# Gathered rows of a graph network summed as three bf16 parts in two half visits, with two blocks fewer gathered

## The chip, the cores and the metric

The kernel runs on one core of one Trainium2 chip. The time is the device time of one execution in microseconds; of the kernel before three runs are on record.

## The reference

The network has 6250 nodes with 256 features and 100000 directed edges. After a layer norm with a ReLU come four layers; in each, every node adds up the rows of its neighbours, and a small perceptron follows:

```python
def agg(h):
    return jax.ops.segment_sum(h[src], dst, num_segments=N)
for l in range(NL - 1):
    h = x + agg(x)
    h = jax.nn.relu(h @ W1s[l] + b1s[l])
    h = jax.nn.relu(h @ W2s[l] + b2s[l])
    x = h @ W3s[l] + b3s[l]
h = x + agg(x)
h = jax.nn.relu(h @ cW1 + cb1)
h = jax.nn.relu(h @ cW2 + cb2)
return h @ cW3 + cb3
```

The input is added to the result at the end. Everything is float32. The edges are the same in all layers and come sorted by `dst`.

## The kernel before

The nodes stand in 49 blocks of 128. In the code, layers are numbered from 0; the text says layer 1 to layer 4, so that layer 1 is `l == 0`. The aggregation of a block of destination nodes is made in one of two ways.

**Dense blocks.** For them a matrix of edge counts (uint8) is built once, in layer 1, out of one-hot matmuls in bf16 (L1271), and stored in HBM. In layers 2 to 4 it is fetched back (`at<-mat`), cast to fp32r tiles `a` by ScalarE and VectorE in turn (L1853; layer 1: L1836), and multiplied on TensorE with the node table `XY`, which holds a high and a low part of each row. Four blocks together make a panel: 49 steps of four matmuls of 512 columns (`agg<-a,XY`, L1962). A panel of three blocks has 384 columns. A block by itself (a solo) takes 49 matmuls of 512 columns with the table as the weights (`agg<-XY,a`, L1877). The tiles `a` come from a ring, so the casts run some steps ahead of TensorE.

**Gathered blocks.** The class `Gathered` holds them, 24, 22, 21 and 19 blocks in the four layers. A block's edges are 16 tiles of 128 edges, and what does not fit there lies in a tile `over` that several blocks share. For each tile an indirect DMA from GpSimd's queue reads the 128 rows of the table that its edges start from (`rows`, issued in `send`, L1631). VectorE builds one-hot matrices `hot` (L1673), one per block. A visit of a block (`add`) sums its tiles on TensorE: every tile is multiplied with a 128x32 one-hot (L1692) into one of four groups of 32 output partitions, which TensorE works on at once. In fp32 each matmul stands in the trace as two records. VectorE then adds the block's own rows (`finish`, L1716 and L1719), TensorE transposes the result (`turned`, L1758), and the perceptron follows (L1448, L1511).

**What sets the order.** The program is written out by a planner. It walks over the steps of the dense product and keeps an estimated time, `clock`, to which each piece of work adds its cost (`VISIT` is 3.0 us, `TURN` 0.4). The gathers of a layer are spread evenly over it (`pace`), each bound to a matmul of TensorE that must have passed; `meets` says when the next visit is due, `TAIL` and `LATE` shift the end of a layer's visits against the end of its dense product. `later(n, f)` writes `f` n steps on. Every engine runs its instructions in the order in which they were written.

**Where the change acts.** In the class `Gathered`, in the two pools of layers 2 to 4 (`rings2` for the tiles `a`, `gath2` for the gathered tiles), and in the tables that say which blocks are dense (`solos`, `slim`, `order`).

Of the kernel before, what the change touches and what calls it, by code (L numbers as in the profile page):

```python
# [17 lines left out]
P = 128  # L18
# [378 lines left out]
def sorted_edges(  # L397
# [61 lines left out]
    ROUNDS = ((3, 1, -1, 0, 4, 2),)  # L459
    CH = 7  # L460
# [12 lines left out]
    solos = [[], [], [], [18, 19]]  # L473
    slim = {1: 1}
# [681 lines left out]
    with tc.manual_schedule():  # L1156
# [157 lines left out]
        def later(n, fn):  # L1314
            due.append((now[0] + n, fn))
# [88 lines left out]
        def bring_inputs(b0, n):  # L1404

            assert layers[NLAYER].sent == len(layers[NLAYER].order)
            assert layers[NLAYER].done == layers[NLAYER].n
            inputs[b0] = [gath.tile([P, C], F32, name="rows") for _ in range(n)]
# [153 lines left out]
        class Gathered:  # L1562
            def __init__(self, l):
# [12 lines left out]
                self.visits = [(g, rounds) for g in range(len(self.blocks)) for rounds in ROUNDS]  # L1576
# [4 lines left out]
                seen_over = set()  # L1581
                for g, rounds in self.visits:
                    b = self.blocks[g][0] + self.blocks[g][2]
                    new = [T] if over_of[b] not in seen_over else []
                    seen_over.add(over_of[b])
                    used_at = {k: i for i, c in reversed([*enumerate(rounds)])
                               for k in range(c, T + 1, 4) if k in (*range(own[b]), *new)}
                    assert len(used_at) == own[b] + len(new)
                    self.order += [(g, k) for k in sorted(used_at, key=lambda k: (used_at[k], k))]
                    self.upto.append(len(self.order))  # L1590

            def meets(self):
# [21 lines left out]

            def send(self, upto):
                while self.sent < min(upto, len(self.order)):
                    g, k = self.order[self.sent]
                    which = over_of[self.blocks[g][0] + self.blocks[g][2]]
                    if k == T:
                        t = gath.tile([P, C], F32, name="over", bufs=2)  # L1620
                        self.shared[which] = t
                        at = late_ends[:, which, 1:2]
                    else:
# [3 lines left out]
                        t = gath.tile([P, C], F32, name="rows")  # L1627
                        self.rows[g, k] = t
# [9 lines left out]
            def advance(self):  # L1638

                if self.first is None:  # L1640
                    return
                self.flow()
                while self.meets():
                    self.send(self.upto[self.done + 1])
                    self.add()
# [10 lines left out]
            def one_hots(self, v):  # L1656
# [5 lines left out]
                if which not in known:  # L1662
                    known.add(which)
                    m = P // Q - 1
                    c = T - 4 * m - min(rounds)
# [5 lines left out]
                shape = [P, len(rounds), P // Q, Q]  # L1671
                self.hot = work.tile(shape, F32, name="hot")
                nc.vector.tensor_tensor(  # L1673
                    self.hot,
                    sums[:, C:C + P].rearrange("p (m q) -> p m q", q=Q)[:, None, :, :].to_broadcast(shape),
                    rel[:, self.blocks[g][3] // T, v % len(ROUNDS), :, :, None].to_broadcast(shape),
                    OP.is_equal)

            def add(self):
# [5 lines left out]
                end = rounds == ROUNDS[-1]  # L1685
                held_by = [[c for c in rounds if 0 <= c + 4 * m < own[b + i] or c + 4 * m == T]
                           for m in range(P // Q)]
                for c in rounds:
                    for m, cs in enumerate(held_by):
                        if c in cs:  # L1690
                            k = c + 4 * m
                            nc.tensor.matmul(  # L1692
                                self.sums[m * Q:(m + 1) * Q, :C],
                                self.hot[:, c - min(rounds), m, :],
                                self.shared[over_of[b + i]] if k == T else self.rows[g, k],
                                start=(c == cs[0]), stop=(c == cs[-1]))
                passed(VISIT)
                self.done += 1
                if self.done < self.n:
                    later(4, lambda v=self.done: self.one_hots(v))  # L1700
# [68 lines left out]
        order = [[], [0, 1, 2, 3, 4, 5, 6], [0, 1, 2, 3, 4, 5, 6], [0, 18, 1, 2, 19, 3, 4, 5, 6]]  # L1769
# [32 lines left out]
        def work_of(l):  # L1802
# [3 lines left out]
            t += len(layers[l].blocks) * (len(ROUNDS) * VISIT + TURN)  # L1806
# [210 lines left out]
        rings = ctx.enter_context(tc.tile_pool(name="rings2", bufs=AHEAD + 5, reuse_waits="tile"))  # L2017
        gath = ctx.enter_context(tc.tile_pool(name="gath2", bufs=27, reuse_waits="tile"))
# [69 lines left out]
```

## Time and profile before

| what | value |
| --- | --- |
| median of three runs | 2338.97 us (2338.20 to 2346.93) |
| the profiled execution | 2345.17 us |
| its span in the trace | 2343.4 us |
| TensorE busy | 2136.8 us, 91% |
| layer 1 / 2 / 3 / 4 in the trace | 92 to 755 / 755 to 1320 / 1320 to 1846 / 1846 to 2343 us |
| blocks gathered in layers 1 / 2 / 3 / 4 | 24 / 22 / 21 / 19 |
| mean granted TensorE clock | 0.973 |

The busy share is that of one engine in the span, and the engines work beside each other. A row of a group reads: line, engine, operation, what is written from what, shape, count, then busy time, the mean of one in ns, and after the second bar the idle time of that engine just before those instructions with what ended it; "issue" there is idle time in which the engine waited for nothing that the profile shows. Matmuls overlap, so the mean of one is longer than the step from one to the next; steps are read from the starts in the timeline.

### The profile page before, as it was taken

What the parts mean: (1) busy time and instruction counts of PE and PEld (TensorE: products, weight loads), DVE (VectorE), ACT (ScalarE), POOL (GpSimd) and SP (SyncE); (2) the same over time, 40 slices, a digit from 0 to 9 for tenths busy, and PEclk for the clock granted to TensorE, in tenths of its full rate; (3) what the DMA queues carried; (4) which work ended last, traced back from release to release, by engine and by line L of the source; (5) the groups of instructions that cost most, each with busy time, mean ns of one, the idle gap of its engine ahead of it and who ended that gap; (6) DMA issues with size and microseconds to landing.
All of it is one profiled execution on the core that took longest, in us unless ns stands there. A gap on an engine that the chain in (4) does not pass through costs nothing.

```text
span 2343.4 us, 33115 instructions
## 1 busy us (share of the span) xinstructions
PE 2136.8 (91%) x12131; PEld 1517.0 (65%) x12131; DVE 909.0 (39%) x2079; ACT 839.3 (36%) x1738; POOL 1398.1 (60%) x1479
## 2 busy tenths in 40 slices
PE   7988898988899999899998999999999999999998
PEld 6766566656567666576666766666666766666665
DVE  8777565666543321222224322222223322322223
ACT  6755454444445322222233322222222422222221
POOL 4466666665551666666666466666666366666664
PEclk9999999999899999999999999999999999999999
DMA  8444444443444644444445544545445554545454
GB/s 240 161 141 129 131 133 122 137 144 119 126 141 138 205 143 121 138 151 145 135 146 184 175 137 118 161 127 156 127 142 179 173 156 151 172 152 178 140 154 125
DMA packets 184921, 348.81 MB, mean 149 GB/s; under 512 B 31785, under 2 KB 118699, under 8 KB 184749
## 3 DMA queue, kind: packets, MB, share of 16 engines
q0 software_dynamic: 68256, 185.33, 27.4%
q1 hardware_dynamic: 115944, 159.42, 20.8%
q10 hardware_dynamic: 548, 1.86, 0.3%
q8 instruction: 97, 1.59, 0.3%
q14 instruction: 76, 0.61, 0.1%
HBM read 287.62 MB, written 58.87 MB: 148 GB/s over the span
## 4 chain that ended last, share of the span: by engine, by line
PE 84%; issue 6%; DVE 3%; another core or an unknown queue 3%; ACT 2%; DMA 1%; POOL 1%; SPq 0%; ACTq 0%; POOLq 0%; DVEq 0%
PE agg L1962 39%; PE sums L1692 14%; PE agg L1877 12%; PE ps L1448 5%; PE ps L1511 5%; PE bp L1271 4%; PE bp L1089 1%; PE ps L1758 1%; DMA rows<-table,idx 1%; DVE hi L1233 1%; DVE at L1281 1%; PE ps L1460 1%; PE ps L1440 0%; POOL rows L1631 0%
## 5 line engine op out<-in xcount | busy, mean ns | idle before, releaser
L1631 POOL DMA_INDIRECT rows<-table,idx x1368 | 1324.5, 968 | 866.2 <-PE agg L1962 279.0
L1962 PE MATMUL agg<-a,XY 128*128 128x512 f32 (+1 forms) x4116 | 986.6, 396 | 11.9 <-issue 5.8
L1962 PEld LDWEIGHTS agg<-a,XY 128*128 128x128 f32 x4116 | 770.4, 190 | 210.3 <-issue 55.2
L1853 ACT CAST a<-at 128x512 fp32r<-128x512 uint8 (+1 forms) x529 | 314.5, 612 | 728.0 <-PE agg L1962 558.2
L1853 DVE CAST a<-at 128x512 fp32r<-128x512 uint8 (+1 forms) x528 | 235.9, 458 | 635.0 <-PE agg L1962 385.0
L1692 PE MATMUL sums<-rows,hot 128*32 128x256 f32 x3768 | 344.3, 391 | 73.8 <-issue 61.5
L1877 PE MATMUL agg<-XY,a 128*128 128x512 f32 x1323 | 384.7, 423 | 3.4 <-issue 1.1
L1692 PEld LDWEIGHTS sums<-rows,hot 128*32 128x32 f32 x3768 | 145.3, 111 | 253.8 <-issue 193.6
L1877 PEld LDWEIGHTS agg<-XY,a 128*128 128x128 f32 x1323 | 240.5, 197 | 47.4 <-issue 6.5
L1279 ACT CAST at<-bp 128x392 uint8<-128x392 f32 x250 | 120.8, 489 | 278.2 <-PE bp L1271 168.5
L1281 DVE CAST at<-bp 128x392 uint8<-128x392 f32 x230 | 129.6, 563 | 221.0 <-PE bp L1271 162.2
L1836 ACT CAST a<-at 128x512 fp32r<-128x512 uint8 (+2 forms) x349 | 190.7, 574 | 7.8 <-PE agg L1877 7.3
L1271 PE MATMUL bp<-hi,lo 128*128 128x196 bf16 x960 | 133.7, 256 | 60.9 <-issue 22.8
L1716 DVE TENSOR_TENSOR sums<-sums,XY 128x256 f32<-128x256 f32 x86 | 37.1, 432 | 345.9 <-PE agg L1962 316.7
L1271 PEld LDWEIGHTS <-lo 128*128 128x128 bf16 x960 | 72.8, 99 | 138.2 <-issue 86.9
L1448 PE MATMUL ps<-h,w 128*128 128x512 f32 (+3 forms) x336 | 139.1, 557 | 12.2 <-ACT h L1762 6.0
L1511 PE MATMUL ps<-w,h 128*128 128x256 f32 x588 | 137.0, 384 | 9.6 <-ACT h L1762 6.2
L1233 DVE TENSOR_TENSOR hi<-cols,pairs 128x784 bf16<-128x784 bf16 x240 | 134.9, 562 | 0.0
L1762 ACT ACTIVATE h<-ps,bias 128x256 f32<-128x256 f32 (+1 forms) x120 | 48.5, 458 | 238.7 <-PE ps L1758 74.0
L1511 PEld LDWEIGHTS ps<-w,h 128*128 128x128 f32 x588 | 112.1, 192 | 28.1 <-ACT h L1762 7.0
L1448 PEld LDWEIGHTS ps<-h,w 128*128 128x128 f32 x336 | 62.4, 195 | 67.9 <-issue 53.2
L1233 DVE TENSOR_TENSOR lo<-lanes,pairs 128x512 bf16<-128x512 bf16 x240 | 100.0, 417 | 0.9 <-PE ps L2008 0.6
(214 smaller groups left out, 1028.1 us busy)
## 6 DMA issues: line engine op xcount, KB each, us to landing
at<-mat SPq DMA_DIRECT2D x149, 448.0 KB
mat<-at SPq DMA_DIRECT2D x30, 784.0 KB
rows<-table,idx POOLq DMA_INDIRECT x1368
table<-zz SPq DMA_DIRECT2D x70, 256.0 KB
back<-table SPq DMA_DIRECT2D x104, 128.0 KB
table<-zs SPq DMA_DIRECT2D x12, 512.0 KB
xt<-in_x_dram SPq DMA_DIRECT2D x22, 256.0 KB
out_dram<-zz SPq DMA_DIRECT2D x22, 256.0 KB
```

Of the source, the lines that this page charges most:

```text
L1233: nc.vector.tensor_tensor(o.rearrange("p q (n t) -> p q n t", t=2), values.rearrange("p (n t) -> p n t", t=2)[:, None, :, :].to_broadcast( ...
L1271: mm = nc.tensor.matmul(bp[:, m * HW:(m + 1) * HW], lo[:, q + m, :], hi[:, q + m, :], start=True, stop=True)
L1279: nc.scalar.copy(o, v)
L1281: nc.vector.tensor_copy(o, v)
L1448: mm = nc.tensor.matmul(ps[:mp, :w], weights[l][0][:, c, i * P:i * P + mp], h1[:, c, :w], start=(c == 0), stop=(c == KC - 1))
L1511: mm = nc.tensor.matmul(o, h2[0][:, c, nodes], w3[:, c, :], start=(c == 0), stop=(c == KC - 1))
L1631: got = nc.gpsimd.indirect_dma_start(out=t, out_offset=None, in_=tables[self.l][:, :], in_offset=bass.IndirectOffsetOnAxis(ap=at, axis=0),)
L1692: nc.tensor.matmul(self.sums[m * Q:(m + 1) * Q, :C], self.hot[:, c - min(rounds), m, :], self.shared[over_of[b + i]] if k == T else self.r ...
L1836: nc.scalar.copy(a[:, i * m * P:(i + 1) * m * P].rearrange("p (j d) -> p j d", j=m), counts[b][:, j:j + m, :])
L1853: cast(o, at[:, n - some:, d:d + m * P])
L1877: mm = nc.tensor.matmul(agg, a[:, d:d + P], XY[:, j, :], start=(j == 0), stop=(j == NT - 1))
L1962: mm = nc.tensor.matmul(agg[c][:, :w], XY[:, j, o:o + P], a[:, :w], start=(at == 0 and half == 0), stop=(at == NT - 1 and half == 1))
```

## The change

In layers 2 to 4 (`if l`) the gathered tiles come four to a tile `rows` of [128, 4, 256], in three buffers; before, each had one of 27 buffers. `send` stops at a four when three are in use; `free` counts them back once they have been split. A new function `halve` splits a four into three bf16 parts: ScalarE copies it to bf16, VectorE subtracts this from the rows, ScalarE copies the rest to bf16, and VectorE subtracts again into the third part. The four operations are written at steps 0, 1, 2 and 3. The tile `over` is split likewise. A visit covers half of a block (`SIDES`, two fours of four tiles each, costed at `HALF` = 1.25), needs both of its fours split, and is written at least `STAND` = 6 steps after that. Its matmuls take the three parts in turn with a bf16 one-hot, all summed in the same fp32 accumulator. One-hots are still built once per block.

Layer 2 gathers 21 blocks instead of 22 (its last panel is now four blocks wide), and layer 3 gathers 20 instead of 21 (block 19 is a solo after panel 2). The ring of `a` in these layers has 7 buffers instead of 8. `TAIL` of layers 2 and 3 goes from -5 to 0, of layer 4 from 8 to 14.

```diff
+    SIDES = ((3, 1, -1), (0, 4, 2))
...
-    solos = [[], [], [], [18, 19]]
-    slim = {1: 1}
+    solos = [[], [], [19], [18, 19]]
+    slim = {}
...
             def meets(self):
 
                 if self.first is None or self.done == self.n or now[0] < self.rest:
                     return False
+                if self.l and now[0] < self.at.get(self.done, now[0]) + STAND:
+                    return False
+                if self.l and self.halved < 2 * (self.done + 1):
+                    return False
...
+            def halve(self):
+
+                while self.halved < min(2 * (self.done + 1), len(self.fours)):
+                    g, c, n, v, upto, which = self.fours[self.halved]
+                    if clock[0] < self.first + (upto - self.upto[1]) * self.pace and (
+                            now[0] < ends[self.l] + LATE[self.l] - STAND):
+                        return
+                    self.send(upto)
+                    assert self.sent >= upto
+                    o = self.parts[g, c] = gath.tile([P, 4, 3, C], BF16, name="parts", bufs=2)
+                    self.three(o[:, :n], self.rows.pop((g, c))[:, :n, :])
+                    self.halved += 1
+                    later(3, self.free)
+                    self.at[v] = now[0]
...
+            def three(self, o, t):
+                nc.scalar.copy(o[:, :, 0, :], t)
+                later(1, lambda: nc.vector.tensor_tensor(t, t, o[:, :, 0, :], OP.subtract))
+                later(2, lambda: nc.scalar.copy(o[:, :, 1, :], t))
+                later(3, lambda: nc.vector.tensor_tensor(o[:, :, 2, :], t, o[:, :, 1, :],
+                                                         OP.subtract))
...
             def send(self, upto):
                 while self.sent < min(upto, len(self.order)):
                     g, k = self.order[self.sent]
+                    if self.l and k < 4 and self.opened >= self.freed + ROWS:
+                        return
...
                 for c in rounds:
-                    for m, cs in enumerate(held_by):
-                        if c in cs:
+                    for h in range(pieces_of):
+                        for m, cs in enumerate(held_by):
                             k = c + 4 * m
+                            if c not in cs:
+                                continue
+                            rows = (self.shared[over_of[b + i]] if k == T else
+                                    self.parts[g, k % 4][:, k // 4] if self.l else self.rows[g, k])
                             nc.tensor.matmul(
-                                self.sums[m * Q:(m + 1) * Q, :C],
-                                self.hot[:, c - min(rounds), m, :],
-                                self.shared[over_of[b + i]] if k == T else self.rows[g, k],
-                                start=(c == cs[0]), stop=(c == cs[-1]))
-                passed(VISIT)
+                                self.sums[m * Q:(m + 1) * Q, :C], self.hot[:, c + 1, m, :],
+                                rows[:, h, :] if self.l else rows, start=(c == cs[0] and h == 0),
+                                stop=(c == cs[-1] and h == pieces_of - 1))
+                passed(HALF if self.l else VISIT)
...
-        TAIL = [16.0] + [-5.0] * (NLAYER - 1) + [8.0]
+        TAIL = [16.0] + [0.0] * (NLAYER - 1) + [14.0]
+        HALF, STAND, ROWS = 1.25, 6, 3
...
-        rings = ctx.enter_context(tc.tile_pool(name="rings2", bufs=AHEAD + 5, reuse_waits="tile"))
-        gath = ctx.enter_context(tc.tile_pool(name="gath2", bufs=27, reuse_waits="tile"))
+        rings = ctx.enter_context(tc.tile_pool(name="rings2", bufs=AHEAD + 4, reuse_waits="tile"))
+        gath = ctx.enter_context(tc.tile_pool(name="gath2", bufs=ROWS, reuse_waits="tile"))
```

How the order of the instructions moves is shown at the start of layer 2. First TensorE before: the first two visits of that layer, each in one piece between stretches of the dense product (`sums` is the accumulator of a gathered block, `agg` that of a panel).

```order
L1962 MATMUL agg<-a,XY 128x512 x128
L1692 MATMUL sums<-rows,hot 32x256 x18
L1692 MATMUL sums<-over,hot 32x256
L1692 MATMUL sums<-rows,hot 32x256 x4
L1962 MATMUL agg<-a,XY 128x512 x76
L1448 MATMUL ps<-h_8937,w_8485 128x512 x4
L1692 MATMUL sums<-rows,hot 32x256 x18
L1692 MATMUL sums<-over,hot 32x256
L1692 MATMUL sums<-rows,hot 32x256 x4
L1962 MATMUL agg<-a,XY 128x512 x44
```

Now, on TensorE, the end of one half visit, the dense product after it, and the start of the next; L2029 is the line of the panel product and L1759 that of the visits. A half is about 34 such pairs of a weight load and a matmul.

```order
L1759 LDWEIGHTS hot
L1759 MATMUL sums<-parts,hot 32x256
L2029 MATMUL agg<-a,XY 128x512 x28
L1451 MATMUL ps<-h_8992,w_8485 128x512 x4
L2029 MATMUL agg<-a,XY 128x512 x16
L1759 LDWEIGHTS hot
L1759 MATMUL sums<-parts,hot 32x256
```

Visits that stood about a hundred matmuls apart in one piece now stand about forty apart in two, and between them the dense product goes on.

Second, ScalarE before at the same place: casts of the counts (`a<-at`) in between the loading of the table (`XY<-back` and `XY<-xt`).

```order
L1853 CAST a<-at 128x512 x3
L1367 CAST XY<-back 128x256 x3
L1367 CAST XY<-xt 128x256 x3
L1853 CAST a<-at 128x512 x3
L1367 CAST XY<-back 128x256 x3
L1367 CAST XY<-xt 128x256 x3
```

Now, on ScalarE, with the two copies of a four (L1657 and L1659) between the casts:

```order
L1920 CAST a<-at 128x512
L1657 CAST parts<-rows 128x4x256
L1920 CAST a<-at 128x512
L1659 CAST parts<-rows 128x4x256
L1920 CAST a<-at 128x512
L1369 CAST XY<-back 128x256 x3
L1369 CAST XY<-xt 128x256 x3
L1920 CAST a<-at 128x512
L1657 CAST parts<-rows 128x4x256
```

The first copy of a four waits for its gathers, and the casts written after it stand behind it in ScalarE's order.

More of the change, by code (lines that the diff above doesn't have):

```diff
@@ L459, in sorted_edges @@
     ROUNDS = ((3, 1, -1, 0, 4, 2),)
+    SIDES = ((3, 1, -1), (0, 4, 2))
+    assert sum(SIDES, ()) == ROUNDS[0] and len(ROUNDS) == 1
     CH = 7
@@ L1407, in bring_inputs @@
             assert layers[NLAYER].done == layers[NLAYER].n
-            inputs[b0] = [gath.tile([P, C], F32, name="rows") for _ in range(n)]
+            together = gath.tile([P, 4, C], F32, name="rows")
+            inputs[b0] = [together[:, i, :] for i in range(n)]
             for i, t in enumerate(inputs[b0]):
@@ L1575, in __init__ @@
                 self.alone = {b + i for b, n, i, _ in self.blocks}
-                self.visits = [(g, rounds) for g in range(len(self.blocks)) for rounds in ROUNDS]
+                self.sides = SIDES if l else ROUNDS
+                self.visits = [(g, rounds) for g in range(len(self.blocks)) for rounds in self.sides]
                 self.n = len(self.visits)
@@ L1642, in advance @@
                 self.flow()
+                if self.l:
+                    self.halve()
                 while self.meets():
@@ L1805, in work_of @@
                  sum(stock[p][1] for p in order[l]) - slim.get(l, 0)) * NT * W * COLS
-            t += len(layers[l].blocks) * (len(ROUNDS) * VISIT + TURN)
+            t += len(layers[l].blocks) * ((2 * HALF if l else VISIT) + TURN)
             for k, n in ((l, NT - tails[l]), (l - 1, tails[l - 1])):
```

58 lines of the change are left out of this document (43 added, 15 removed).

## The prediction

> **What bounds the kernel now.** I read the engine totals and the chain of the page first, then the windows view with one stretch per layer (92:755 is layer 1, the other three are layers 2 to 4), then the costliest groups and a timeline of single visits.
>
> ```profile
> PE 2136.8 (91%) x12131; PEld 1517.0 (65%) x12131; DVE 909.0 (39%) x2079; ACT 839.3 (36%) x1738; POOL 1398.1 (60%) x1479
> PE 84%; issue 6%; DVE 3%; another core or an unknown queue 3%; ACT 2%; DMA 1%; POOL 1%; SPq 0%; ACTq 0%; POOLq 0%; DVEq 0%
> core 0: us, PE busy (x) PEld busy (x) DVE busy (x) ACT busy (x) POOL busy (x), PEclk, DMA share, GB/s
> 92.00:755.00 663.00, 590.42 (x3738) 408.57 (x3737) 396.25 (x922) 337.92 (x789) 386.03 (x395) 0.96 0.44 133
> 755.00:1320.00 565.00, 516.12 (x2797) 369.60 (x2797) 160.82 (x345) 161.07 (x315) 343.75 (x357) 0.98 0.49 151
> 1320.00:1846.00 526.00, 491.48 (x2609) 345.38 (x2609) 132.34 (x282) 140.31 (x258) 327.72 (x340) 0.98 0.48 147
> 1846.00:2343.00 497.00, 460.54 (x2575) 327.16 (x2573) 149.16 (x313) 133.26 (x245) 298.19 (x308) 0.98 0.51 158
> ```
>
> TensorE sets the end: 91% busy, 84% of the chain. Layers 2 to 4 last 565 + 526 + 497 = 1588 us, and VectorE and ScalarE are busy there for 442 and 435 us, 28% and 27%. The change touches only these layers and spends that idle time. What it wants to shorten are the visits of the gathered blocks. The same view for L1692 alone gives the busy time of the visits by layer, and the groups give TensorE's idle time ahead of their instructions (first pair layer 1, second pair layers 2 to 4).
>
> ```profile
> 92.00:755.00 663.00, 77.05 (x1100) 37.01 (x1100) 0.96 0.44 133
> 755.00:1320.00 565.00, 97.69 (x1008) 39.93 (x1008) 0.98 0.49 151
> 1320.00:1846.00 526.00, 93.69 (x962) 38.68 (x962) 0.98 0.48 147
> 1846.00:2343.00 497.00, 79.88 (x870) 31.54 (x870) 0.98 0.51 158
> L1692 PE MATMUL sums<-rows,hot 128*32 128x256 f32 x1052 | 76.8, 384 | 6.0 <-issue 5.4
> L1692 PE MATMUL sums<-over,hot 128*32 128x256 f32 x48 | 14.4, 381 | 0.3 <-issue 0.3
> L1692 PE MATMUL sums<-rows,hot 128*32 128x256 f32 x2716 | 267.5, 394 | 67.8 <-issue 56.2 <-DMA rows<-table,idx 3.0
> L1692 PE MATMUL sums<-over,hot 128*32 128x256 f32 x124 | 40.9, 397 | 3.4 <-issue 2.5
> ```
>
> Layer 1 spends (77.05 + 6.3)/24 = 3.47 us on a block, layers 2 to 4 (271.26 + 71.2)/62 = 5.52 us, for the same 46 matmul records. The timeline shows an undisturbed visit (990.34 to 993.07, 2.73 us) and a stretched one (1210.33 to 1218.59, 8.26 us).
>
> ```profile
> 990.34 2.14 PE L1692 MATMUL sums<-rows,hot 128*32 128x256 f32 x35
> ...
> 993.07 3.28 PE L1962 MATMUL agg<-a,XY 128*128 128x512 f32 x13
> 1210.33 2.22 PE L1692 MATMUL sums<-rows,hot 128*32 128x256 f32 x26
> 1213.33 0.67 PE L1692 MATMUL sums<-rows,hot 128*32 128x256 f32 x4 [0.78 <-issue]
> 1214.77 0.59 PE L1692 MATMUL sums<-rows,hot 128*32 128x256 f32 x2 [0.77 <-issue]
> 1216.17 0.38 PE L1692 MATMUL sums<-rows,hot 128*32 128x256 f32 x1 [0.81 <-issue]
> ...
> 1218.59 3.74 PE L1962 MATMUL agg<-a,XY 128*128 128x384 f32 x20
> ```
>
> The stretched one starts as fast as the other and then gets a few matmuls every 0.7 or 1.4 us, with nothing awaited that the profile shows ("issue"). I call this the stall: (5.52 − 2.73) × 62 = 173 us in layers 2 to 4. What causes it I could not read from the trace, and its fate decides the sign.
>
> **The change part by part.**
>
> *The summing on TensorE.* A block has 23 matmuls. In fp32 each is two records; after, each is three bf16 matmuls, 69 for a block, in two visits. Prices come from a timeline in layer 1:
>
> ```profile
> 299.69 3.40 PE L1511 MATMUL ps<-w,h 128*128 128x256 f32 x15
> 302.93 0.50 PE L1271 MATMUL bp<-hi,lo 128*128 128x196 bf16 x4
> 303.22 1.18 PE L1877 MATMUL agg<-XY,a 128*128 128x512 f32 x4
> 304.24 0.67 PE L1271 MATMUL bp<-hi,lo 128*128 128x196 bf16 x4
> 304.69 1.63 PE L1877 MATMUL agg<-XY,a 128*128 128x512 f32 x6
> ```
>
> Start to start, an fp32 record of 256 columns takes 3.24/15 = 0.216 us. Four quadrants run at once, so 46 records need 46/4 × 0.216 = 2.48 us, and 2.73 − 2.48 = 0.25 us is entering and leaving the mode. A bf16 matmul of 196 columns takes 0.29/4 = 0.073 or 0.45/4 = 0.113 us, which scaled to 256 columns is 0.095 to 0.147. I take half of an fp32 record, 0.108, near the lower end, because neighbours in other quadrants can hide a weight load. A block then needs 69/4 × 0.108 + 2 × 0.25 = 2.36 us (ends 2.14 and 3.03). Undisturbed, 62 × 2.73 = 169.3 becomes 60 × 2.36 = 141.6: **−28 us** (ends −41 and +13). The Trainium skill, "TensorEngine Tiling (Array Packing)", Key Properties, speaks against the two visits: changing the tiling mode drains TensorE. The trace agrees that a switch costs something, the 0.25 us above; 60 more switches are in the sum at +15 us.
>
> *The stall.* The row nearest to the new visits is the old visit at the same places in the same layers, 2.79 us over 2.73. I scale it with the undisturbed time: 2.79 × 2.36/2.73 = 2.41, 60 × 2.41 = 145 instead of 173, **−28 us**. The ends lie far apart: layer 1's 3.47 − 2.73 = 0.74 a block gives 44 us (−129); a full stall in each half, 5.58 a block, gives 335 us (+162).
>
> *The two blocks less.* Layer 2's last panel grows from three blocks to four, layer 3 gets one block by itself.
>
> ```profile
> L1962 PE MATMUL agg<-a,XY 128*128 128x512 f32 x3902 | 944.5, 399 | 10.0 <-issue 5.8 <-ACT a L1853 3.1
> L1962 PE MATMUL agg<-a,XY 128*128 128x384 f32 x196 | 36.2, 340 | 0.0
> L1877 PE MATMUL agg<-XY,a 128*128 128x512 f32 x98 | 23.5, 394 | 1.2 <-issue 1.1
> L1758 PE MATMUL ps<-ident,u 128*128 128x128 f32 x124 | 18.9, 273 | 0.9 <-DVE zz L1519 0.8 <-DVE u L1719 0.2
> ```
>
> Per matmul that is 944.5/3902 = 0.242 against 36.2/196 = 0.185, so widening costs 196 × 0.057 = 11.2 us; the lone block is 49 × (23.5 + 1.2)/98 = 12.4 us; two block turns saved are 2 × 18.9/62 = 0.6. Together **+23 us**, all on TensorE. The two visits saved are in the 62 against 60 above.
>
> *The splitting.* Four tiles take two ScalarE copies and two VectorE subtractions, 234 of each of the four operations (and 18 of each for the `over` tiles, 128x256). The nearest rows are casts and differences of the same 1024 elements:
>
> ```profile
> L1112 ACT CAST XY<-zs 128x1024 fp32r<-128x1024 f32 x12 | 12.7, 1054 | 1.6 <-DVE zs L1099 1.6
> L1117 DVE TENSOR_TENSOR XY<-zs,XY 128x1024 fp32r<-128x1024 f32 x12 | 14.6, 1220 | 4.4 <-ACT XY L1112 4.4
> L1853 ACT CAST a<-at 128x512 fp32r<-128x512 uint8 x485 | 292.8, 620 | 698.8 <-PE agg L1962 540.4 <-issue 66.6 <-remote 46.6
> L1853 DVE CAST a<-at 128x512 fp32r<-128x512 uint8 x499 | 221.1, 454 | 609.6 <-PE agg L1962 371.9 <-issue 69.2 <-remote 68.5
> ```
>
> That is 468 × 1.054 = 493 us more on ScalarE and 468 × 1.220 = 571 us more on VectorE, before the small ones. With 435 and 442 there now, they become about 58% and 64% busy in 1588 us. Both engines also cast the counts (`a`) for TensorE, which waited only 3.1 us for these casts. Casts run several steps of 4 × 0.242 us ahead, which covers one copy of 1.05 us or one difference of 1.22, so I book no wait inside a layer. If the cover were gone, it would be up to 234 × 1.05 = 246 us. Where a layer ends, the last four's chain, 2 × (1.054 + 1.220) = 4.5 us, stands ahead of the last visit: 3 × 4.5 = 13.6 at most, 0 at least. I take half: **+7 us**.
>
> *The gathers and the one-hots.* A gather now waits for VectorE to release one of three fours, and twelve tiles can be under way instead of 27.
>
> ```profile
> L1631 POOL DMA_INDIRECT rows<-table,idx x382 | 373.0, 976 | 241.9 <-issue 70.9 <-PE bp L1271 56.5 <-PE agg L1877 53.1
> L1631 POOL DMA_INDIRECT rows<-table,idx x986 | 951.5, 965 | 624.3 <-PE agg L1962 279.0 <-issue 195.4 <-remote 52.5
> ```
>
> GpSimd has 624 us to spare in layers 2 to 4 (second row). The Trainium skill, "SBUF — State Buffer", Who interferes with whom, states that a VectorE instruction with two SBUF inputs contends with a GpSimd instruction that reads SBUF; all the added subtractions have two, and by that rule up to 571 us of the gathers' slack would go. The trace has no such price: with VectorE 60% busy in layer 1 (396 of 663) a gather takes 976 ns, with 28% 965. I book 0 for the gathers. The one-hot stays one per block on VectorE, off TensorE's path.
>
> **Sum**: −28 − 28 + 23 + 7 = −26 us. The profiled execution took 2345.17 us, so it would take 2319; from the median of 2338.97 that is **2313 us**. Its own range, from the price of a bf16 matmul (−13 to +41 us) and the layer ends (±7), is 2293 to 2361, and I call it 2290 to 2360.
>
> **The rivals.**
>
> *The short visits lose the stall* (0.13). If the stall belongs to a long run of fp32 records, short bf16 halves fall to layer 1's 0.74 a block: −28 − 129 + 23 + 7 = −127, **2212 us**. For it: stretched visits begin at full pace and stall only after 26 records, more than a half would have in four-pass terms. Against: the releases of ScalarE and VectorE also come late near visits, so the lateness may start ahead of them.
>
> *Each half meets the stall anew* (0.15). If what is late is TensorE's own completion, and a visit merely runs into it with its many short instructions, 120 entries pay what 62 did: −28 + 162 + 23 + 7 = +164, **2503 us**; half of it 2421. It decides for slower when a half stalls by more than (173 + 28 − 23 − 7)/120 = 1.43 us. For it: the stall is "issue", not a tile; a half has 69 instructions with its weight loads in 1.2 us, a block now 92 in 2.73. Against: 120 entries, but each with half of the time to lose.
>
> *TensorE issues no more records than now* (0.07). Layers 2 to 4 go from 7981 matmuls (2797 + 2609 + 2575) to about 7981 − 2840 + 4140 + 49 = 9330. At layer 1's 3738/663 = 5.64 per us that needs 1654 us instead of 1588: **2405 us**. Against: layer 1's own pace need not be a limit.
>
> *Casts queue behind the splitting* (0.14). The first copy waits for a gather to land, with casts behind it in ScalarE's order, and the ring of `a` is one shorter. A quarter microsecond lost per four is 234 × 0.25 = 58: −26 + 58, **2371 us**. For it: 12 tiles in flight are under one block. Against: the 624 us of slack.
>
> *The weight loads of 32 columns aren't hidden* (0.06): the upper price 3.03 instead of 2.36 is +40, **2353 us**, no change.
>
> **How the numbers follow.** The forecast has 0.45. A change of 0.5% is 11.7 us, about what a measurement of this kernel can tell from none. Faster (under 2327): 0.28 of the forecast's 0.45, 0.13 of the lost stall, 0.04 of the mild ends of the others, 0.45. Same (2327 to 2351): 0.13 of the forecast, 0.03 of the weight loads, 0.05 of mild waits, 0.21. Slower: 0.04 of the forecast and the rest of the rivals, 0.34. The range leaves out the deep ends of the lost stall and of the doubled one: 2225 to 2415.
>
> **What would show it.** Right: L1759 busy plus idle near 60 × 4.77 = 286 us in layers 2 to 4, the rest of TensorE's rows +23 us, waits for `a` under 10 us. The lost stall shows as L1759 near 190; the doubled one as over 450, with "issue" ahead of it; the casts as idle of the L2029 group put down to ScalarE or VectorE. The prediction is wrong if the stall per half is under 0.5 or over 1.5 us, or if waits for `a` pass 25 us.

## The result and the profile after

The changed kernel takes 2496.54 us (median of four runs, 2490.15 to 2500.22) against 2342.29 us for the kernel before in the same comparison: 1.066 times as long, 95% interval 1.063 to 1.070. The prediction of 2313 us and its range up to 2415 us are both missed, on the slower side.

The kernel before does not take the same time on every chip: about 2340 us on the chip of the traces in the prediction, 2373 us on a second one, and 2020 to 2022 us on three others. So every ratio below is against the kernel before on the same chip.

The windows view of the changed kernel, cut at its own layer ends, has layers 2 to 4 in 603, 594 and 538 us; in the kernel before they lasted 565, 526 and 497.

```profile
92.00:753.00 661.00, 591.40 (x3767) 410.64 (x3766) 399.22 (x932) 341.33 (x798) 386.47 (x396) 0.97 0.45 135
753.00:1356.00 603.00, 519.39 (x3231) 379.43 (x3230) 341.49 (x518) 320.26 (x489) 369.94 (x340) 0.95 0.45 138
1356.00:1950.00 594.00, 498.70 (x3078) 364.62 (x3077) 316.18 (x467) 297.60 (x441) 348.98 (x325) 0.93 0.42 129
1950.00:2488.00 538.00, 455.03 (x2964) 330.62 (x2962) 312.10 (x462) 273.11 (x398) 335.67 (x308) 0.94 0.47 143
```

TensorE's busy time there is 1473 us, against 1468 before. What grew is the time in which it is not busy: 1735 − 1473 = 262 us against 120. No engine looks full. VectorE and ScalarE are at 56% and 51%, and GpSimd, by its busy time, at 61%. The granted clock fell from 0.98 to between 0.93 and 0.95, and a matmul of a four-block panel has a mean of 413 ns (L2029 below) against 399 before (L1962).

TensorE's groups in layers 2 to 4 show where it now waits.

```profile
L2029 PE MATMUL agg<-a,XY 128*128 128x512 f32 x4076 | 1054.5, 413 | 77.4 <-ACT a L1920 43.0 <-issue 22.7 <-ACT parts L1657 8.1
L1759 PE MATMUL sums<-parts,hot 128*32 128x256 bf16 x3942 | 182.2, 292 | 115.5 <-DVE parts L1660 47.1 <-ACT parts L1659 31.9 <-issue 22.7
L1759 PE MATMUL sums<-over,hot 128*32 128x256 bf16 x180 | 34.1, 297 | 2.8 <-DVE parts L1660 1.0 <-issue 0.8 <-ACT a L1920 0.4
L1824 PE MATMUL ps<-ident,u 128*128 128x128 f32 x120 | 22.5, 299 | 39.4 <-DVE u L1785 23.5 <-DVE sums L1782 15.2 <-DVE zz L1500 0.8
```

The matmuls of the visits became cheaper, but TensorE waits for the split parts (about 80 us), for the casts of the counts (43 us) and for VectorE's finishing of blocks (39 us). All these stand in ScalarE's and VectorE's order behind the splitting. ScalarE's waits say what the splitting itself stands still for (waited for, us in total, times, longest):

```profile
ACT parts L1657 <- DMA rows<-table,idx: 302.7, 69, 10.8
```

One such wait in the timeline (start, duration, engine, idle time before in brackets):

```profile
1564.26 2.35 DVE L1660 TENSOR_TENSOR parts<-rows,parts 128x1024 bf16<-128x1024 f32 x2
...
1566.21 1.22 POOL L1686 DMA_INDIRECT rows<-table,idx  x1 [4.65 <-issue]
...
1574.27 0.94 POOL L1686 DMA_INDIRECT rows<-table,idx  x1 [0.30 <-issue]
1575.52 0.95 POOL L1686 DMA_INDIRECT rows<-table,idx  x1 [0.30 <-issue]
1577.97 1.04 ACT L1657 CAST parts<-rows 128x1024 bf16<-128x1024 f32 x1 [8.59 <-DMA rows<-table,idx]
1578.92 0.61 ACT L1920 CAST a<-at 128x512 fp32r<-128x512 uint8 x1
1579.05 1.23 DVE L1658 TENSOR_TENSOR rows<-rows,parts 128x1024 f32<-128x1024 f32 x1 [8.41 <-ACT parts L1657]
...
1580.53 2.35 DVE L1660 TENSOR_TENSOR parts<-rows,parts 128x1024 bf16<-128x1024 f32 x2
1580.54 0.40 PE L1759 MATMUL sums<-parts,hot 128*32 128x256 bf16 x4 [6.32 <-ACT parts L1659]
...
1582.48 1.22 POOL L1686 DMA_INDIRECT rows<-table,idx  x1 [6.01 <-issue]
```

It reads as a circle. VectorE writes the third parts (L1660), the last operation that reads a four. GpSimd, idle for 4.65 us until then, begins to gather into the freed buffer. (The profile names only "issue" as the end of that wait; that it was for the buffer is read from the times.) Its gathers start at least 1.25 us apart. The one beside L1660 takes 1.22 us, the last two, while VectorE waits, 0.94 and 0.95. When the last has landed, ScalarE's copy (L1657) ends a wait of 8.59 us; casts come after it; VectorE's subtraction ends a wait of 8.41 us, TensorE one of 6.32 us, and GpSimd, again idle for 6.01 us, gets the next buffer.

### The profile page after: what moved, and what is told of

It reads as the page before. It is cut to its first block, busy times and chain, and to the rows that moved or that the text cites. A ratio compares the mean times of both kernels' runs of the same rounds, so it can differ in the third digit from the quotient of the medians.

```text
span 2488.4 us, 37254 instructions
## 1 busy us (share of the span) xinstructions
PE 2142.7 (86%) x13452; PEld 1551.4 (62%) x13452; DVE 1439.8 (58%) x2596; ACT 1299.0 (52%) x2258; POOL 1483.6 (60%) x1446
## 5 line engine op out<-in xcount | busy, mean ns | idle before, releaser
L1686 POOL DMA_INDIRECT rows<-table,idx x1336 | 1408.9, 1055 | 916.2 <-issue 398.0
L2029 PE MATMUL agg<-a,XY 128*128 128x512 f32 x4116 | 1064.7, 413 | 79.2 <-ACT a L1920 43.0
L2029 PEld LDWEIGHTS agg<-a,XY 128*128 128x128 f32 x4116 | 794.3, 197 | 315.1 <-issue 77.4
L1658 DVE TENSOR_TENSOR rows<-rows,parts 128x1024 f32<-128x1024 f32 (+1 forms) x240 | 291.7, 1218 | 586.0 <-ACT parts L1657 374.5
L1657 ACT CAST parts<-rows 128x1024 bf16<-128x1024 f32 (+1 forms) x240 | 249.0, 1040 | 647.0 <-DMA rows<-table,idx 302.7
L1944 PE MATMUL agg<-XY,a 128*128 128x512 f32 x1372 | 400.1, 423 | 7.7 <-issue 4.4
L1660 DVE TENSOR_TENSOR parts<-rows,parts 128x1024 bf16<-128x1024 f32 (+1 forms) x240 | 288.4, 1223 | 59.6 <-ACT parts L1659 40.3
L1759 PE MATMUL sums<-parts,hot 128*32 128x256 bf16 x3942 | 182.2, 292 | 115.5 <-DVE parts L1660 47.1
L1659 ACT CAST parts<-rows 128x1024 bf16<-128x1024 f32 (+1 forms) x240 | 243.8, 1038 | 68.7 <-DVE rows L1658 52.6
L1920 DVE CAST a<-at 128x512 fp32r<-128x512 uint8 x535 | 215.8, 425 | 66.8 <-PE agg L2029 47.6
L1759 PEld LDWEIGHTS <-hot 128*32 128x32 bf16 x4122 | 112.6, 100 | 198.2 <-issue 171.2
```

The costliest lines, as they stand in the source:

```text
L1657: nc.scalar.copy(o[:, :, 0, :], t)
L1658: later(1, lambda: nc.vector.tensor_tensor(t, t, o[:, :, 0, :], OP.subtract))
L1659: later(2, lambda: nc.scalar.copy(o[:, :, 1, :], t))
L1660: later(3, lambda: nc.vector.tensor_tensor(o[:, :, 2, :], t, o[:, :, 1, :], OP.subtract))
L1686: got = nc.gpsimd.indirect_dma_start(out=t, out_offset=None, in_=tables[self.l][:, :], in_offset=bass.IndirectOffsetOnAxis(ap=at, axis=0),)
L1759: nc.tensor.matmul(self.sums[m * Q:(m + 1) * Q, :C], self.hot[:, c + 1, m, :], rows[:, h, :] if self.l else rows, start=(c == cs[0] and h ...
```

## The experiments

Theory 1 was: the waits for gathers are the loss, through the order of ScalarE and VectorE. Its rivals: the work of the splitting itself (2), the two visits (3), the regrouping (4).

**Fixed rows.** The splitting reads a tile that is always there, and what the first subtraction leaves goes to a tile of its own, in bf16; the gathers go on, and nobody reads them.

```diff
...
-                nc.scalar.copy(o[:, :, 0, :], t)
-                later(1, lambda: nc.vector.tensor_tensor(t, t, o[:, :, 0, :], OP.subtract))
-                later(2, lambda: nc.scalar.copy(o[:, :, 1, :], t))
...
+                t, rest = fixed[0].to_broadcast([P, n, C]), fixed[1][:, :n, :]
+                nc.scalar.copy(o[:, :, 0, :], t)
+                later(1, lambda: nc.vector.tensor_tensor(rest, t, o[:, :, 0, :], OP.subtract))
+                later(2, lambda: nc.scalar.copy(o[:, :, 1, :], rest))
...
```

> The changed kernel, but the splitting reads a fixed tile instead of the gathered rows (the gathers are still made, nobody reads them, and the sums are those of the fixed tile). Same operations on every engine, no wait of ScalarE for a gather and none of a gather for VectorE. Theory 1 (ScalarE's first copy waits at the head of its queue for gathers, and the casts, the finishes and the splitting behind it come late): the time falls from 2496 to 2300 to 2340 us. Theory 2 (the added 1064 us of work on ScalarE and VectorE are too much beside the casts, with or without waiting): it stays above 2440. Theory 3 (the two short visits and their stalls cost): it stays above 2470.

Measured: 2387.61 us, ratio 1.007 (1.005 to 1.009) on a chip where the kernel before takes 2373. The absolute expectation was set for another chip; as a ratio theory 1 expected 0.98 to 1.00, and the other two over 1.04. It came near theory 1: without the waits most of the loss is gone, as far as a ratio from this chip can be set against the 1.066 from another.

**No splitting.** The half visits read one fixed tile of parts.

```diff
...
-                    o = self.parts[g, c] = gath.tile([P, 4, 3, C], BF16, name="parts", bufs=2)
-                    self.three(o[:, :n], self.rows.pop((g, c))[:, :n, :])
...
+                    self.parts[g, c] = fixed[0]
+                    self.rows.pop((g, c))
...
```

> The changed kernel without the splitting: the half visits read one fixed tile of bf16 parts, gathers are made but not read, ScalarE and VectorE have only their old work. Theory 1 and theory 2: 2280 to 2330 us, and what it lies below the run with the fixed rows is the price of the sheer work, under 15 us by theory 1 and over 100 by theory 2. Theory 3: above 2470 us, since the visits are the same. A half takes 1.1 to 1.3 us undisturbed.

Measured: 2407.70 us, ratio 1.017 (1.011 to 1.022), on the same chip. That is above the fixed rows, so the sheer work on ScalarE and VectorE costs nothing that shows on this chip, and theory 2 falls as it was put. But the time is far above what theory 1 expected. As I read the groups of this run, the time that the visits save appears ahead of the panels' matmuls as "issue".

```profile
L2035 PE MATMUL agg<-a,XY 128*128 128x512 f32 x4077 | 1066.6, 410 | 90.8 <-issue 82.3 <-DVE a L1926 2.3 <-ACT h L1834 1.1
L1765 PE MATMUL sums<-parts,hot 128*32 128x256 bf16 x4122 | 166.8, 276 | 56.5 <-issue 46.1 <-DVE hot L1741 10.1
```

**Half visits in fp32.** Two visits, no splitting, six fours in flight, one-hots in fp32, and a half visit costed at 1.5 in the planner.

```diff
-                    o = self.parts[g, c] = gath.tile([P, 4, 3, C], BF16, name="parts", bufs=2)
-                    self.three(o[:, :n], self.rows.pop((g, c))[:, :n, :])
+                    self.parts[g, c] = self.rows.pop((g, c))
...
-                pieces_of = 3 if self.l else 1
+                pieces_of = 1
...
```

> The changed kernel without the splitting, the two half visits summing the gathered fp32 rows themselves (six fours in flight instead of three). Theory 1: dense work +23 us and 60 more switches of 0.25 us, so 2342 + 23 + 15 = 2380 us with the stall as before, less if short visits meet less of it. Theory 3 (each half meets the stall anew, 2.8 us): 2342 + 23 + 15 + 160 = 2540 us.

Measured: 2292.21 us, ratio 0.965 (0.961 to 0.969). Theory 3 falls: two visits do not double the stall.

**The regrouping alone**, in the kernel before.

```diff
-    solos = [[], [], [], [18, 19]]
-    slim = {1: 1}
+    solos = [[], [], [19], [18, 19]]
+    slim = {}
...
```

> The kernel before with only the two blocks moved from the gathered to the dense part. The sum in the prediction gives +23 us of dense work less two visits of 5.5 us: 2342 + 12 = 2354 us. Theory 4 (the regrouping upsets the planner's timing) would give over 2390 us.

Measured: 2330.57 us, ratio 0.982 (0.978 to 0.987), faster although it adds dense work. Theory 4 falls, and so does my price of +12 us on this chip. The fp32 halves have this regrouping too, so about half of their gain is not due to the two visits: 2292.21 against 2330.57 us is 0.984.

The next four ran where the kernel before takes 2021.46 us.

**Gathers asked for earlier.**

```diff
-                self.pace = (self.end - clock[0] - MARGIN) / self.upto[-1]
-                self.lead = MARGIN + self.upto[1] * self.pace
+                ahead = 12.0 if self.l else MARGIN
+                self.pace = (self.end - clock[0] - ahead) / self.upto[-1]
+                self.lead = ahead + self.upto[1] * self.pace
```

> The changed kernel with the gathers of layers 2 to 4 asked for 12 us of the planner's time ahead of the first copy instead of 6. With the fixed rows the time was 1.007 of before, against 1.066 with gathered ones, so theory 1 says that some 140 us hang on gathers that land after ScalarE has come to their copy. If 6 us of lead are what is missing, the ratio falls to between 1.01 and 1.03; if the three buffers hold the gathers back (theory 1b), it stays above 1.05.

Measured: 2326.19 us, ratio 1.151 (1.149 to 1.153). More lead does not help: the ratio of the changed kernel itself, measured later where the kernel before takes 2022 us, is 1.136. That the three buffers keep the gathers from using the lead fits theory 1b, but this run does not show it.

**Four fours for the gathers.**

```diff
-        HALF, STAND, ROWS = 1.25, 6, 3
+        HALF, STAND, ROWS = 1.25, 6, 4
...
-                        o = gath.tile([P, 1, 3, C], BF16, name="over3", bufs=2)
+                        o = gath.tile([P, 1, 3, C], BF16, name="over3", bufs=1)
```

> The changed kernel with four fours for the gathers instead of three (paid for with one buffer of the split over tile). Theory 1b (the release of a four by VectorE holds the next gathers back): the ratio to before falls from 1.066 to 1.03 or less. Theory 1 with the lead alone: over 1.05.

Measured: 2168.55 us, ratio 1.073 (1.071 to 1.075). Taken against 1.066 it looks like no gain, but the two ratios come from different chips. The changed kernel had to be run on such a chip as well.

**Fewer pieces.** The kernel without the splitting, with two matmuls for each tile or one instead of three.

```diff
-                pieces_of = 3 if self.l else 1
+                pieces_of = 2 if self.l else 1
```

> The kernel without the splitting, with two bf16 matmuls for each tile instead of three: 1374 matmuls and as many weight loads fewer. Theory 5 (TensorE pays for every instruction that it has to get through, wherever the delay shows): no_split lay 115 us over the fp32 halves with 1374 matmul records more, so this one comes to within 20 us of the fp32 halves, ratio 0.96 to 0.975. Theory 6 (bf16 halves cost for another reason than their number): only the matmuls' own time goes, 1374 x 0.027 = 37 us, ratio 1.00.

> The same with one bf16 matmul for each tile: 2748 matmuls and weight loads fewer than no_split. Theory 5: another 100 us less, ratio 0.91 to 0.93. Theory 6: 74 us less than no_split, ratio 0.985.

Measured: 1973.47 us (ratio 0.976, 0.975 to 0.978) and 1941.84 us (0.960, 0.959 to 0.962). Both expectations were worked out for a chip with the stall, and the run without the splitting was not made on this one. The step between the two is 32 us, near the 37 us of the matmuls themselves. On this chip no "issue" shows, so nothing is learned on theory 5 for the chips that stall.

The third group put both kernels on one chip, on which the kernel before takes 2022 us.

**Both kernels, the fixed rows and the fp32 halves again.**

> The kernel before, for a trace on the chip of this group. The groups so far ran on different chips and the kernel before took 2342, 2373 and 2021 us there; where it took 2021, no row of the traces named issue as what TensorE waited for. Theory 7 (the stall belongs to the chip or to the moment, and the program only decides where it shows): if this chip takes near 2021, layer 1 takes some 570 us instead of 670, a visit 2.7 us everywhere and the issue waits are gone. If the time is again near 2350, visits stall as in the first trace.

> The changed kernel on the same chip. Theory 1 (the waits for the gathers cost what they cost, about 300 us, and on the first chip half of that fell into time in which TensorE would have stalled anyway): without the stall the ratio to before is about 1.13 to 1.16, with it about 1.066 again. If theory 1 is wrong and the loss adds to the stall, the ratio without it is 1.075.

> The fixed rows on the same chip, no wait for a gather. Theory 1: without the stall within 3% of before on either side; what lies between this and the changed kernel is the price of the waits, 200 us or more without the stall, 140 with it.

> The two half visits in fp32 on the same chip. If the shorter visits gain only by missing the stall, then without it this one lies 23 us of dense work and 60 switches of 0.25 us over before less two visits of 2.7 us, 30 us, ratio 1.015; with the stall 0.965 again.

Measured: 2020.43, 2295.24, 2081.94 and 2049.58 us; ratios 1.000, 1.136 (1.134 to 1.138), 1.030 (1.028 to 1.032) and 1.014 (1.012 to 1.015). The windows view of the kernel before on this chip:

```profile
92.00:661.00 569.00, 557.18 (x3763) 395.05 (x3762) 396.36 (x932) 342.36 (x797) 388.27 (x395) 1.00 0.51 156
661.00:1131.00 470.00, 466.92 (x2770) 353.33 (x2769) 154.76 (x334) 158.20 (x305) 344.43 (x357) 1.00 0.57 179
1131.00:1589.00 458.00, 456.23 (x2642) 340.13 (x2641) 139.65 (x291) 145.74 (x264) 326.98 (x340) 1.00 0.55 171
1589.00:2018.00 429.00, 418.47 (x2545) 313.40 (x2543) 146.85 (x306) 131.98 (x239) 298.85 (x308) 0.99 0.57 181
```

The changed kernel, cut near its layer ends:

```profile
661.00:1231.00 570.00, 506.57 (x3238) 376.21 (x3237) 342.80 (x520) 321.38 (x493) 368.08 (x340) 0.95 0.47 147
1231.00:1790.00 559.00, 486.70 (x3075) 363.63 (x3074) 317.18 (x467) 297.81 (x441) 342.94 (x325) 0.93 0.45 136
1790.00:2285.00 495.00, 434.69 (x2965) 325.54 (x2963) 312.11 (x463) 273.53 (x399) 342.00 (x308) 0.95 0.50 155
```

In the kernel before, layer 1 takes 569 us instead of 663, TensorE is busy for 99% of layers 2 to 4, and no visit stalls. So the stall belongs to the chip or the moment, and theory 7 stands. Four fours (1.073) about halve the loss, whose ratio is 1.136 here, and the waits for gathers are worth 2295 − 2082 = 213 us. The loss does not add to the stall: 273 us here, 154 us where TensorE would have stalled anyway.

In the changed kernel on this chip, layers 2 to 4 are 267 us longer (1624 against 1357). Of these, 181 are idle time of TensorE (196 against 15) and 86 are busy time (1428 against 1342), at a granted clock of 0.93 to 0.95 instead of 0.99 to 1.00. The panels' matmuls (L2029) are busy for 1021 us, against 976 in the run with the fixed rows on the same chip. What lowers the clock was not tested.

The fixed rows still lost 3%, at the edge of what was expected. Up to 2004 us of its trace, with all copies and subtractions in place, TensorE is busy for 1332 of the 1343 us of layers 2 to 4 at a clock of 1.00. The loss is all at one place, in the waits of that run:

```profile
PE agg L1443 <- DVE h L2047: 61.7, 1, 61.7
```

At its end everything else was done, and GpSimd was still gathering. The gathers' rows in layers 2 to 4 of four kernels on such chips (busy, mean of one, idle before), first the kernel before:

```profile
L1631 POOL DMA_INDIRECT rows<-table,idx x986 | 951.7, 965 | 394.6 <-issue 161.3 <-PE agg L1962 157.7 <-DMA w<-in_L_gnn_W2s_dram 40.7
```

The changed kernel:

```profile
L1686 POOL DMA_INDIRECT rows<-table,idx x954 | 1033.3, 1083 | 572.8 <-issue 256.2 <-PE agg L2029 113.9 <-DVE a L1920 68.3
```

The fixed rows:

```profile
L1694 POOL DMA_INDIRECT rows<-table,idx x954 | 1091.0, 1144 | 331.1 <-issue 170.6 <-PE agg L2037 72.5 <-ACT XY L1369 40.7
```

Four fours:

```profile
L1686 POOL DMA_INDIRECT rows<-table,idx x954 | 1083.3, 1136 | 394.0 <-issue 137.2 <-PE agg L2029 97.5 <-DVE a L1920 63.4
```

Gathers that follow each other directly have 0.30 us between them, so 0.30 us for each of them is no spare time. That leaves 394.6 − 296 = 99 us of real idle time before, 572.8 − 286 = 287 in the changed kernel, and 45 with the fixed rows: there GpSimd hardly rests, and bounds the kernel. A gather takes 965 ns before and 1083 to 1144 with the splitting. This gave theory 8: GpSimd's gathers bound layers 2 to 4, because VectorE's subtractions lengthen them and because they wait for buffers.

**No subtractions; the same with four fours; the same with the fixed rows.**

```diff
                 nc.scalar.copy(o[:, :, 0, :], t)
-                later(1, lambda: nc.vector.tensor_tensor(t, t, o[:, :, 0, :], OP.subtract))
                 later(2, lambda: nc.scalar.copy(o[:, :, 1, :], t))
-                later(3, lambda: nc.vector.tensor_tensor(o[:, :, 2, :], t, o[:, :, 1, :],
-                                                         OP.subtract))
...
```

> The changed kernel without VectorE's two subtractions (the second part is a copy of the rows, the third is the second again). Theory 8 (GpSimd's gathers became what bounds layers 2 to 4: each is longer while VectorE subtracts, 1084 ns against 965, and they wait 247 us for the release of the three fours): a gather takes 965 ns again, and the release comes some 2.5 us earlier in each four, so on a chip on which before takes 2021 us the ratio falls from 1.136 to between 1.03 and 1.07; on one where it takes 2350, from 1.066 to 1.00 to 1.03. Theory 9 (a gather is longer for another reason): it stays at 1080 ns.

> Four fours for the gathers and no subtractions: the two causes of theory 8 both taken away. Four fours alone gave 1.073 where before took 2021 us. By theory 8 the gathers then have no long waits, GpSimd needs 970 x 1.28 = 1240 us, under TensorE's 1340, and the ratio is 0.99 to 1.02 (0.96 to 1.01 on a chip with the stall). If casts behind the copies cost by themselves, it stays above 1.04.

> The fixed rows without the subtractions. With them GpSimd never rested, a gather took 1142 ns, and the last gathers ended 62 us after everything else. Theory 8: 965 ns, no such tail, ratio 0.995 to 1.01 where before takes 2021 us.

Measured, where the kernel before takes 2020.88: 2047.98, 2016.18 and 2008.42 us; ratios 1.013 (1.011 to 1.015), 0.998 (0.997 to 0.999) and 0.994 (0.992 to 0.995). The gathers in the first of them:

```profile
L1683 POOL DMA_INDIRECT rows<-table,idx x954 | 921.8, 966 | 448.4 <-issue 164.9 <-PE agg L2026 102.9 <-ACT parts L1658 65.9
```

A gather takes 966 ns again, as theory 8 has it and theory 9 does not, and the ratio fell further than expected (1.03 to 1.07). With four fours the loss is gone altogether, as expected, and the fixed rows came a little under what was expected. Taking away VectorE's subtractions and adding a fourth buffer together removes the whole loss.

**Two parts.** A version made from this: one copy and one subtraction for a four, two matmuls for a tile, five fours for the gathers, a four given back two steps earlier, and a half visit costed at 0.9 in the planner.

```diff
                 nc.scalar.copy(o[:, :, 0, :], t)
-                later(1, lambda: nc.vector.tensor_tensor(t, t, o[:, :, 0, :], OP.subtract))
-                later(2, lambda: nc.scalar.copy(o[:, :, 1, :], t))
-                later(3, lambda: nc.vector.tensor_tensor(o[:, :, 2, :], t, o[:, :, 1, :],
-                                                         OP.subtract))
+                later(1, lambda: nc.vector.tensor_tensor(o[:, :, 1, :], t, o[:, :, 0, :],
+                                                         OP.subtract))
...
```

> A version made from theory 8: the rows are split into two bf16 parts instead of three (one copy on ScalarE, one subtraction on VectorE for a four; the bits below the second part are dropped), two matmuls for a tile, and the room goes into five fours for the gathers. Half of the subtractions make a gather 1025 ns, GpSimd needs 970 x 1.33 = 1290 us, under TensorE's 1330: ratio 0.98 to 1.00 where before takes 2021 us, 0.94 to 0.98 on a chip with the stall.

Measured: 2076.67 us, ratio 1.029 (1.026 to 1.032). That is outside the expected 0.98 to 1.00. A gather is 1055 ns instead of 1025, and its idle time beyond the gaps is 390.5 − 286 = 104 us:

```profile
L1684 POOL DMA_INDIRECT rows<-table,idx x954 | 1006.9, 1055 | 390.5 <-issue 113.2 <-PE agg L2027 110.1 <-DMA w<-in_L_gnn_W2s_dram 65.7
```

One subtraction for a four lengthens the gathers by three quarters of what two do (90 ns of 118). No version that sums all the gathered rows was shown to beat the kernel before on both kinds of chip: the fp32 halves do by 3.5% where it stalls, and are 1.4% slower where it does not; the regrouping alone was run only where it stalls.

## Why the prediction was wrong, point by point

*What bounds the kernel.* TensorE, yes; but I took GpSimd's 624 us of idle time in layers 2 to 4 for slack. 986 × 0.30 = 296 us of it are fixed gaps. At 1.25 us from one gather to the next, 1005 gathers (986 for `rows`, 19 for `over`) would need 1256 us by my estimate, 79% of the 1588 us in the trace that I read, and 93% of the 1357 us that these layers take without the stall. GpSimd was the second bound, and its share of busy time, 61% of the 1588 and 71.5% of the 1357 us, did not show it.

*The step that failed* is "I book 0 for the gathers", together with "no wait inside a layer" for the casts. In the profile after, TensorE waits 80 us for split parts, 43 for casts and 39 for finished blocks, 162 us in all, where 7 were booked. The runs without the stall show what is behind it. Of the 273 us lost there, taking the subtractions away gave back 247 us, a fourth buffer 127 us, and both 279 us, measured by the ratios. In the changed kernel the gathers are 82 us longer in all (1033.3 − 951.7, for 32 fewer), and GpSimd's idle time beyond the gaps grows by 188 us. That these two come near the loss shows nothing by itself, since busy and idle time of one engine always fill the layers; it says how GpSimd spent the time. I take the subtractions to act twice, by lengthening gathers and by holding back the release of a four; the two effects were not taken apart. Their mere load on VectorE is no third: the fixed rows keep it, and TensorE hardly waits there before the tail.

The Trainium skill had the rule: "SBUF — State Buffer", Who interferes with whom, says that a VectorE instruction with two SBUF inputs contends with a GpSimd instruction that reads SBUF. I set layer 1's row against it (976 ns with VectorE 60% busy). That row averages over other VectorE instructions; with these subtractions, fp32 over 1024 elements, a gather takes 1083 to 1144 ns, and without them 965 to 967. The run agrees with the rule in direction, and it gives the size.

*The rivals.* "Casts queue behind the splitting" came nearest in mechanism, with its circle through the twelve tiles in flight, but its price of 58 us was far too low. "Each half meets the stall anew" named 2503 us, next to the 2496 measured, and is wrong all the same: visits in halves took 0.965 of the time of before in fp32 (0.984 of the regrouping alone), and L1759 with its idle time is 182.3 + 118.3 = 301 us, not over 450. That this is near the 286 us of the forecast is luck: of the 118.3 only 23.5 are "issue", and 80 are the waits for split parts. The sign that did hold is the one for being wrong, waits for `a` over 25 us: they are 43. "TensorE issues no more records than now" falls where there is no stall: four fours without subtractions take 0.998 with all the records. Where there is one, the run without the splitting (1.017 against 0.965 of the fp32 halves, with 1374 matmuls more) leaves it open.

*The summing* came out a little better than predicted. The windows view cut to the visits of layers 2 to 4, where nothing stalls, for the kernel before:

```profile
661.00:2018.00 1357.00, 177.95 (x2840) 90.54 (x2840) 1.00 0.56 177
```

For the fp32 halves:

```profile
662.00:2049.00 1387.00, 181.04 (x2748) 80.78 (x2748) 1.00 0.55 170
```

And for the bf16 halves with fixed rows and no subtractions:

```profile
662.00:2007.00 1345.00, 139.91 (x4122) 103.15 (x4122) 1.00 0.56 176
```

The bf16 halves take 139.9 us; predicted were 141.6, with the weight loads hidden. A block takes 181.04/60 = 3.02 us in two fp32 visits and 177.95/62 = 2.87 in one, so the second entry costs 0.15 us and not the 0.25 that I took, 9 us in all instead of 15. The Trainium skill's rule of the drain, "TensorEngine Tiling (Array Packing)", Key Properties, is not contradicted, but its price is small here.

*The stall.* Shorter visits seem to lose part of it, as that rival said (the 0.984), but it is not TensorE's alone to lose: with the splitting away and the bf16 halves left, it appeared in front of the dense product. That it belongs to the chip or the moment, and is 320 us of the 2342, I could not know from one trace. What it is stays open: no run found its cause.

*The two blocks*: the same view for the panels alone, first before, then with the bf16 halves, fixed rows and no subtractions:

```profile
661.00:2018.00 1357.00, 960.55 (x4081) 755.37 (x4079) 1.00 0.56 177
```

```profile
662.00:2007.00 1345.00, 973.82 (x4075) 754.34 (x4073) 1.00 0.56 176
```

That is 13.3 us more for the widening, where 11.2 were predicted. *The splitting's own work* cost TensorE nothing, as booked: 0.994 with all the copies. Its subtractions cost through the gathers. *The layer ends* were not measured by themselves.

## What to carry to other kernels

Price a queue of gathers from start to start, not by its busy share, and hold that against the time of the stage: an engine that is busy for 71.5% of a stage can be at 93% of its pace. A step put between a load and its use makes the load's buffers wait for two more engines, and puts a wait at the head of their queues; count buffers against the length of that circle. And before a rule is set aside with an average, look whether the instructions in the average are the ones that the change adds.

## What the runs showed that I had not expected

The same program takes 2342 and 2373 us on two chips and 2020 to 2022 on three others, and nothing in the profile names the reason: on the first two the matmuls of a visit come, for a while, in steps of about 0.7 us or twice that with "issue" in front. The granted clock does not make up for it: 0.973 and 0.997 in the traces of the kernel before, 2.4% apart, where the times are 16% apart. A change that makes TensorE wait looks half as bad there (154 us) as elsewhere (273 us), and the fp32 halves gain there (0.965) and lose elsewhere (1.014). About half of that gain is the regrouping's: alone, although it adds dense work, it was 1.8% faster there.
